# Four graph layers with residual and layer norm: denominators read back behind the last stores, residuals in idle buffers, counts loaded ahead, pieces made by ScalarE

## The chip, the cores and the metric

The kernel runs on one core of a Trainium2 chip. The metric is the device time of one execution in microseconds. The kernel before was run five times: the median is 3411.24 us, the lowest 3408.18, the highest 3414.22. One execution was also profiled; every duration below comes from it.

The engines are called by their short names: PE is TensorE, DVE is VectorE, ACT is ScalarE, POOL is GpSimd and SP is SyncE, which here only issues transfers. PSUM is the memory that PE writes to.

## The reference

`x` is 3327 x 512 in float32, `adj` is 3327 x 3327 of 0 and 1. Four layers follow each other, each of the form `x = layernorm(x + L(x, adj))`:

```python
# layers 0, 2 (8 heads of 64) and 3 (4 heads of 128); layers 2 and 3 end with elu
Wh = x @ W[h];  f1 = Wh @ a1;  f2 = Wh @ a2
e = leaky_relu(f1[:, None] + f2[None, :], 0.2)
att = softmax(where(adj > 0, e, -9e15), axis=1)
L = concat_h(att @ Wh)
# layer 1
keep = (adj > 0) & (cumsum(adj > 0, axis=1) <= 64)
cnt = keep.sum(1)
xj = leaky_relu((keep @ x) / max(cnt, 1) @ Wn.T + bn)
xi = leaky_relu(x @ Wl.T + bl)
L = xi + where(cnt > 0, xj, 0)
```

## The kernel before

**Tiles.** Rows and columns are padded to 26 tiles of 128 (`NT`), and two halves of 13 tiles (`HALF`, 1664 columns, `IW`). The mask (`adj` transposed, fp8) stays in SBUF for all layers. Weighted values go through DRAM (`vd`), as do the unnormalised outputs (`hd`).

**Attention (layers 0, 2, 3).** `Layer.unit` (L361) is one half of the query columns with one of four groups of heads: two heads in layers 0 and 2, one in layer 3. So a layer has eight units, (half, s) = (0, 0) to (1, 3). A unit goes over the 26 key tiles `j`. For each key tile and head, DVE makes the weights `t` from the row terms `rb` and the mask (L402), ACT makes from `t` an fp8 indicator `y`, whether the score is above zero (L405), and PE multiplies `t` with the values `vj` into `po` (L425, from L413). The softmax's denominators are split off: PE sums `y` and the mask against small bf16 "pieces" (`sden`, `sm`) into `pd` (`den`, L375 and L377), two key tiles after the `t`. The pieces are the bf16 parts of the exponentials of the columns, made by `cut` (L321), one call for each half.

**Jobs.** A unit returns a list of small jobs, which the next unit takes one for each key tile: the outputs turned by PE (`pt`, L453), copied by ACT to `hb` (L457) and stored by SP to `hd` (L458). At the end of a half, `pd` holds the sums of all heads; DVE turns it with four transposes into `db` (L486, L487) and reduces it (L491) to `red`. SP writes `red` in four transfers of 32-byte pieces to `dd` (L495) and reads it back in one, with the layout changed, as `pes` (L498); `finish_sums` (L500 on) makes the reciprocals `rec` on DVE from it (L507, L511, L513). The last unit of layer 3 does this with PE instead (`sums`, 13 matmuls with a constant `c1w`, L533). In unit (0, 0) `prepare` and `cut` for the second half are among the jobs, in layer 0 also the counts of neighbours by tile (`count_jobs`, L612: PE counts into `pct`, DVE casts to `ct` at L629, PE sums the tiles before into `pn` at L631, DVE clamps it at L632, stores it to `ctd` and finds the empty columns `nb` at L635). The second half's counts are in unit (0, 2).

**Passages.** `finish_steps` (L165) ends a layer for two row tiles: it loads `h` from `hd` and the residual `xr` (L126 is the line of both loads), divides by `rec` (L180), for elu an exponential `e` (L185), adds (L191, L192, L194), and `norm_rows` (L144) takes the statistics (L152, L153) and scales (`rs` at L154 to L158, `h` at L161). Tiles 0 and 1, which need the first half only, are finished ahead inside the last unit (`ending`, L434).

**Layer 1.** `sage` (L645) has two stages. In the first, for each row tile, PE turns `h` (L682), ACT copies it to `xT` (L684), PE multiplies by both weights (`pz` L690, `pi` L693); `pz` is split into three bf16 parts, of which two, `zs`, stay in SBUF and the third goes through DRAM (`zd`, L700); `xi` is stored (L705). In the second, `kept` (L770, L774) makes the 0/1 tiles `kt` of neighbours to keep from a running count, with carries `cy` loaded by POOL (L659) and added by ACT (L762); PE sums `acc` over 26 key tiles and three parts (L809), the third from `zl`, loaded at L727; `output` (L778) divides by the counts `cnt` (from `cb`, L741 to L745) and finishes a row tile (first step `y`, L782). Layer 2's projection is done between, as jobs, with `wsb` (L730). Layer 3's projection is in `third` (L822 on), with `pt` (L258) and `pw` (L268).

**What sets the order.** PE runs in the order of the program text. For the other engines a scheduler sets a fixed order when the kernel is built, except for instructions pinned by `keep_in_program_order`. Each engine runs its order strictly in turn. Transfers by SP go round eight queues' semaphores, and a transfer may carry a wait for the one eight before it.

Of the kernel before, what the change touches and what calls it, by code (L numbers as in the profile page):

```python
# [18 lines left out]
P = 128  # L19
# [13 lines left out]
def kernel(  # L33
# [131 lines left out]
    def finish_steps(pool, xin, layer, t0, n, hbufs=6, eng=nc.sync, xbufs=None):  # L165
        H, D = layer.H, layer.D
        ys, xs, steps = [], [], []

        def load():
            for t in range(t0, t0 + n):  # L170
                h = pool.tile([P, F], F32, name="h", bufs=hbufs)
                load_tile(h, hd, t, eng)
                ys.append(h)
                xr = pool.tile([P, F], F32, name="xr", bufs=xbufs)
                load_tile(xr, xin, t, nc.gpsimd)
                xs.append(xr)

        def divide(s):
            h = ys[s]
            nc.vector.tensor_tensor(h.rearrange("p (h d) -> p h d", h=H), h.rearrange("p (h d) -> p h d", h=H),  # L180
                                    rec[:, t0 + s, :H].rearrange("p (h e) -> p h e", e=1).to_broadcast([P, H, D]),
                                    op=ALU.mult)
            if layer.elu:
                e = pool.tile([P, F], F32, name="e")
                nc.scalar.activation(e, h, AF.Exp)  # L185
                xs.append(e)

        def add(s):
            h, xr = ys[s], xs[s]
            if layer.elu:  # L190
                nc.vector.scalar_tensor_tensor(xr, xs[n + s], 1.0, xr, op0=ALU.min, op1=ALU.add)  # L191
                nc.vector.scalar_tensor_tensor(h, h, 0.0, xr, op0=ALU.max, op1=ALU.add)  # L192
            else:
                nc.vector.tensor_tensor(h, h, xr, op=ALU.add)  # L194

        steps.append(load)
        for s in range(n):
            steps += [lambda s=s: divide(s), lambda s=s: add(s)]
        steps.append(lambda: norm_rows(pool, ys, t0))
        return ys, steps  # L200
# [22 lines left out]
    class Layer:  # L223
# [97 lines left out]
        def cut(self, pool, half, tag="pc", bufs=1, pinned=False):  # L321
# [7 lines left out]
            for c0 in (0, 3):  # L329
                if c0:  # L330
                    nc.vector.tensor_tensor(dc, dc, qc, op=ALU.mult)
                ins = nc.vector.tensor_copy(pc[:, :, :, c0], dc)
                if pinned:
                    tc.keep_in_program_order(ins)
                nc.vector.tensor_tensor(rest, dc, pc[:, :, :, c0], op=ALU.subtract)
                nc.vector.tensor_copy(pc[:, :, :, c0 + 1], rest)
                nc.vector.tensor_tensor(rest, rest, pc[:, :, :, c0 + 1], op=ALU.subtract)
                nc.vector.tensor_copy(pc[:, :, :, c0 + 2], rest)
# [6 lines left out]
            for k in range(HS):  # L345
                m = self.sm[:, ts, 32 * k:32 * k + 32].rearrange("p t (s c) -> p t s c", c=8)
                for c0, f in ((0, -0.5), (3, -1.0)):
                    nc.vector.tensor_scalar(m[:, :, :, c0:c0 + 3], pc[:, :, k::HS, c0:c0 + 3], f, None,
                                            op0=ALU.mult)
# [11 lines left out]
        def unit(self, pools, half, s, background, aside, final=None, ending=None):  # L361
# [72 lines left out]
            if ending:  # L434
                ending()
# [46 lines left out]
            if not (final and s == NS - 1):  # L482
# [9 lines left out]
                dd = dram.tile([IW, 2, 2 * NS], F32, name=f"dd{self.li}{half}{s}")  # L492
                for kk in range(4):
                    i_, w_ = (0, WA) if kk < 2 else (WA, WB)
                    nc.sync.dma_start(out=dd[i_:i_ + w_, kk % 2, :].rearrange("(b i) x -> i b x", i=32),  # L495
                                      in_=red[32 * kk:32 * kk + 32, :w_ // 32].rearrange("p b o s -> p b (o s)"))
                pes = sp.tile([P, HALF, 2, 2, NS], F32, name="pes", tag="red", bufs=1)
                nc.sync.dma_start(out=pes.rearrange("p q k o s -> p q (k o s)"),  # L498
                                  in_=dd.rearrange("(q p) k x -> p q (k x)", p=P))
# [15 lines left out]
                jobs += [nothing] * max(0, 6 - len(jobs))  # L515
                at = 6 if half == 0 or s < NS - 1 else len(jobs)
                if final and s > 1:

                    return [nothing] * 5 + [finish_sums] + jobs[2:]
                return jobs[:at] + [finish_sums] + jobs[at:]  # L520

            for c in range(2):
                nc.scalar.copy(db[:64, c * (WA // 2):(c + 1) * (WA // 2)], pd[c][:64, :WA // 2])
                nc.vector.tensor_copy(db[64:, c * (WB // 2):(c + 1) * (WB // 2)], pd[c][64:, :WB // 2])
            held = []

            def sums():

                pe = po[0][:, :2 * HALF * H].rearrange("p (q o h) -> p q o h", q=HALF, o=2)
                held.append(pe)  # L530
                for q in range(HALF):
                    e = int(q >= NA)
                    nc.tensor.matmul(pe[:, q, :, :], db[:, (q - e * NA) * P:(q - e * NA + 1) * P], c1w[:, :, e, :],  # L533
                                     start=True, stop=True)

            def reciprocals():
                pe = held[0]
                nc.vector.tensor_tensor(r_[:, :, 0, ss], pe[:, :, 0, ss], rc[:, :, 0, ss], op=ALU.mult)
                nc.vector.tensor_tensor(r_[:, :, 0, ss], pe[:, :, 1, ss], r_[:, :, 0, ss], op=ALU.add)
                nc.vector.reciprocal(rec[:, t0:t0 + HALF, hs], rec[:, t0:t0 + HALF, hs])  # L540


# [69 lines left out]
    def count_jobs(pool, half):  # L612
        jobs = []
        for s0, n in QUADS:
# [12 lines left out]
            def none(i0=i0, w_=w_, held=held):  # L627
                ct = pool.tile([P, 4 * P], BF, name="ct", bufs=1)
                nc.vector.tensor_copy(ct[:, :w_], held["p"][:, :w_])  # L629
# [5 lines left out]
                nc.vector.tensor_scalar(nb[:, :w_], pn[:, :w_], 0.0, None, op0=ALU.is_equal, saturate=False)  # L635
# [9 lines left out]
    def sage(first, first_pool, xin, prev, nxt, wsrc, dst):  # L645
# [3 lines left out]
        with tc.tile_pool(name="sg_z", bufs=1, reuse_waits="tile") as zp, \  # L649
# [20 lines left out]
            with tc.tile_pool(name="sa_w", bufs=1, reuse_waits="tile") as wp, \  # L670
# [35 lines left out]

                pend = None
# [12 lines left out]
            with tc.tile_pool(name="sb_w", bufs=1, reuse_waits="tile") as wp, \  # L720
# [9 lines left out]
                load_wide(wsb, wsrc, nc.gpsimd)  # L730
                nc.vector.tensor_copy(wsb[:, :, :, FW:], wa[nxt.li].rearrange("p c (e h) -> p c e h", e=2))
# [7 lines left out]

                cb = wp.tile([P, NT], BF, name="cb")  # L740
                nc.gpsimd.dma_start(out=cb, in_=ctd[NT:NT + 1, :].rearrange("o (t p) -> p (o t)", p=P))  # L741
                cnt = wp.tile([P, 3, NT], F32, name="cnt")
                nc.vector.tensor_scalar(cnt[:, 0, :], cb, NEIGHBOURS, 1.0, op0=ALU.min, op1=ALU.max)
                nc.vector.reciprocal(cnt[:, 1, :], cnt[:, 0, :])
                nc.vector.tensor_scalar(cnt[:, 2, :], cb, 0.0, None, op0=ALU.is_gt)  # L745
# [53 lines left out]
                for b in range(len(blocks)):  # L799
# [3 lines left out]
                    for s in range(G):  # L803
                        acc = ps.tile([P, F], F32, name="acc", bufs=2)
                        for t in range(NT):
                            if b == 0 and len(kts) < NT and t % 2 == 0:
                                kts += kept(0, len(kts))
                            for c in range(3):
# [7 lines left out]
                            if jobs and (t == 11 and t0 + s > 1 or t == 17):  # L816
                                jobs.pop(0)()
                        y = output(acc, t0 + s)
# [172 lines left out]
    with tc.tile_pool(name="col0", bufs=1) as cp, tc.tile_pool(name="raw", bufs=2) as rawp, \  # L991
# [63 lines left out]
        def first_jobs(pool, half, s):  # L1055
# [6 lines left out]
            if (half, s) == (0, 1):  # L1062
                jobs = []
                for li, wT, a in ((2, w2T, a2), (3, w3T, a3)):
# [10 lines left out]
                     ending=lambda: ends.extend(finish(f0, x, L0, 0, 2, 2)))  # L1075

    with tc.tile_pool(name="col2", bufs=1) as cp:
# [3 lines left out]
        with tc.tile_pool(name="fin2", bufs=1, side="right") as f2:  # L1081
            ends = []
            with tc.tile_pool(name="at_r2", bufs=3, reuse_waits="tile") as rp, \
# [7 lines left out]
                             ending=lambda: ends.extend(finish(f2, x2, L2, 0, 2, 2)))  # L1091
# [47 lines left out]
```

## Time and profile before

| | |
|---|---|
| median of five runs | 3411.24 us |
| profiled execution | 3414.22 us, span 3412.0 us, mean granted PE clock 0.982 |
| layer 0's projection, mask | 0 to 140 us |
| layer 0's attention, 8 units | 140 to 960 us |
| layer 1, first stage | 960 to 1171 us |
| layer 1, second stage, with layer 2's projection | 1171 to 1776 us |
| layer 2's attention | 1776 to 2568 us |
| layer 3's projection | 2568 to 2716 us |
| layer 3's attention | 2716 to 3380 us |
| tail | 3380 to 3412 us |

The stages' borders are read from the first and last instructions of their lines in the timeline. In the rows of groups, a line, an engine, an operation and its tiles come first, then busy time, mean ns of one and the idle time of the engine just before, with what ended it. In a timeline row the start, the duration (of several merged instructions where the count at the end is over one), and in square brackets the idle time ahead of it and what it waited for.

### The profile page before, as it was taken

The numbers are of one execution on the slowest core, as the hardware profiler recorded it, in microseconds if no ns is written. First come the engines' busy times: TensorE is split into PE (matmuls) and PEld (weight loads), VectorE is DVE, ScalarE is ACT, GpSimd is POOL, SyncE is SP. The second block draws the span as 40 slices with busy tenths as digits, with TensorE's granted clock in tenths as the row PEclk, the third lists the DMA queues.
The fourth block names the chain that finished last, engine by engine and source line by source line (L and its number), as shares of the span: only waits on it lengthen the run. The fifth ranks groups of instructions, "written<-read, shape, count | busy, mean of one in ns | idle before, by whom it ended". The sixth has DMA issues, their size and how long they took to land.

```text
span 3412.0 us, 46967 instructions
## 1 busy us (share of the span) xinstructions
PE 3267.9 (96%) x18371; PEld 1633.4 (48%) x18423; DVE 2695.9 (79%) x2630; ACT 2351.8 (69%) x2128; POOL 216.3 (6%) x344
## 2 busy tenths in 40 slices
PE   8899999999989899999989999999997999999997
PEld 7534344444434345545544444444445754445453
DVE  6799999999967544444449999999997766668886
ACT  2388998999943233333338999899996755559885
POOL 3100000000010111111110000000001000000000
PEclk9899999999989999999999999999998999999998
DMA  9544111111143433333320111111107411122311
GB/s 380 208 131 120 49 49 53 46 45 30 36 129 123 124 102 90 87 87 85 83 80 25 42 50 48 56 45 46 35 25 224 169 41 42 41 51 79 95 42 48
DMA packets 313365, 284.65 MB, mean 83 GB/s; under 512 B 134253, under 2 KB 248631, under 8 KB 313144
## 3 DMA queue, kind: packets, MB, share of 16 engines
q1 hardware_dynamic: 280584, 170.27, 17.0%
q0 software_dynamic: 27040, 103.70, 9.7%
q10 hardware_dynamic: 5520, 7.69, 0.7%
q8 instruction: 145, 2.38, 0.3%
q14 instruction: 76, 0.62, 0.1%
HBM read 212.22 MB, written 69.35 MB: 83 GB/s over the span
## 4 chain that ended last, share of the span: by engine, by line
PE 81%; DVE 7%; issue 5%; DMA 4%; ACT 2%; SPq 0%; POOL 0%; ACTq 0%; DVEq 0%; POOLq 0%
PE po L425 49%; PE acc L809 12%; PE pd L377 7%; PE pw L268 5%; DVE t L402 4%; PE pz L690 3%; PE pi L693 3%; DMA raw<-in_adjT_dram 2%; PE pk L770 1%; PE pt L453 1%; ACT y L405 1%; PE pa L1022 0%; PE pt L258 0%; DVE mask L593 0%; DMA cy<-ctd 0%
## 5 line engine op out<-in xcount | busy, mean ns | idle before, releaser
L402 DVE SCALAR_TENSOR_TENSOR t<-rb,qc,mask 128x1664 f32<-128x1664 f32 x1040 | 1959.9, 1960 | 167.4 <-PE po L425 149.9
L405 ACT ACTIVATE y<-t,bi,sc 128x1664 fp8e4<-128x1664 f32 x1040 | 1771.2, 1766 | 317.8 <-PE pd L377 304.9
L425 PE MATMUL po<-t,vj 128*64 128x448 f32 (+3 forms) x8320 | 1927.0, 520 | 25.1 <-DVE t L402 22.2
L425 PEld LDWEIGHTS po<-t,vj 128*64 128x64 f32 (+1 forms) x8320 | 847.7, 148 | 981.4 <-issue 691.6
L809 PE MATMUL acc<-zs,kt 128*128 128x512 bf16 x1312 | 396.9, 382 | 2.2 <-issue 0.2
L809 PEld LDWEIGHTS <-kt 128*128 128x128 fp8e4 x2028 | 199.7, 98 | 252.4 <-issue 11.4
L268 PE MATMUL pw<-wsb,xT 128*128 128x264 f32 (+1 forms) x1248 | 303.4, 399 | 5.8 <-DVE vt L274 4.2
L762 ACT CAST pk<-cy 128x512 f32<-128x512 bf16 x169 | 99.0, 587 | 298.9 <-DVE kt L774 253.1
L268 PEld LDWEIGHTS pw<-wsb,xT 128*128 128x128 f32 x1248 | 242.8, 198 | 51.2 <-ACT qc L272 3.2
L377 PE MATMUL pd<-y,sden 128*32 128x448 fp8e4 (+1 forms) x4160 | 259.3, 341 | 8.2 <-ACT y L405 8.2
L809 PE MATMUL acc<-zl,kt 128*128 128x512 bf16 x664 | 253.1, 381 | 5.6 <-DMA zl<-zd 4.9
L774 DVE SCALAR_TENSOR_TENSOR kt<-pk,mask 128x512 fp8e4<-128x512 f32 x169 | 116.0, 687 | 102.1 <-PE pk L770 102.1
L377 PEld LDWEIGHTS <-sden 128*32 128x32 bf16 x4160 | 117.3, 96 | 160.5 <-issue 137.6
L274 DVE TENSOR_TENSOR vt<-pw,dc 128x256 f32<-128x256 f32 x156 | 59.1, 419 | 145.2 <-ACT dc L269 141.7
L356 POOL DMA_DIRECT2D rb<-r x40 | 21.2, 532 | 1618.6 <-DVE t L402 1604.4
L272 ACT COPY rc<-pw 128x8 f32<-128x8 f32 (+1 forms) x78 | 12.7, 163 | 137.5 <-PE pw L268 137.5
L690 PE MATMUL pz<-wn,xT 128*128 128x512 f32 x208 | 98.7, 619 | 9.1 <-ACT xT L684 9.1
L693 PE MATMUL pi<-wl,xT 128*128 128x512 f32 x208 | 93.5, 592 | 0.0
L659 POOL DMA_DIRECT2D cy<-ctd x91 | 67.9, 746 | 340.4 <-ACT pk L762 312.2
L154 ACT ACT_TABLE_LOAD x45 | 57.7, 1283 | 37.3 <-DVE mv L153 36.7
L782 DVE SCALAR_TENSOR_TENSOR y<-acc,cnt,bnb 128x512 f32<-128x512 f32 x26 | 19.5, 751 | 80.0 <-PE acc L809 80.0
L593 DVE TENSOR_SCALAR mask<-raw 128x832 fp8e4<-128x832 int32 (+2 forms) x90 | 52.9, 598 | 36.1 <-DMA raw<-in_adjT_dram 36.0
(177 smaller groups left out, 1665.5 us busy)
## 6 DMA issues: line engine op xcount, KB each, us to landing
vj<-v SPq DMA_DIRECT2D x312, 128.0 KB
rb<-r POOLq DMA_DIRECT2D x40, 832.0 KB, 4.7
raw<-in_adjT_dram SPq DMA_DIRECT2D x67, 416.0 KB
cy<-ctd POOLq DMA_DIRECT2D x78, 256.0 KB, 4.0
h<-hd SPq DMA_DIRECT2D x61, 256.0 KB
v<-vt SPq DMA_DIRECT2D x50, 256.0 KB
hd<-hb SPq DMA_DIRECT2D x48, 256.0 KB
xr<-x POOLq DMA_DIRECT2D x45, 256.0 KB, 3.2
```

The costliest lines, as they stand in the source:

```text
L268: nc.tensor.matmul(pw[e][:, :FW + H], xT[:, c, :], wsb[:, c, e, :], start=c == 0, stop=c == FC - 1)
L274: nc.vector.tensor_tensor(vt[:, hs, :], pw[e][:, :FW].rearrange("p (h d) -> p h d", d=D), self.dc[:, t, hs].rearrange("p (h e) -> p h e", e=1)
L377: nc.tensor.matmul(pd[c][32 * kk:32 * kk + 32, :w_], lhsT, rhs, start=(kk, c) not in seen, skip_group_check=final is not None, stop=last a ...
L402: nc.vector.scalar_tensor_tensor(t, rb[k], self.qc[:, j, h:h + 1], mask[:, j, i0:i0 + IW], op0=ALU.max, op1=ALU.mult)
L405: nc.scalar.activation(y, t, AF.Sigmoid, bias=self.bi[:, j, h:h + 1], scale=self.sc[:, j, h:h + 1], saturate=False)
L425: nc.tensor.matmul(po[c][k * D:(k + 1) * D, :z - a_], vj[:, j % 2, k * D:(k + 1) * D], ts[k][:, a_:z], start=j == 0, stop=j == NT - 1)
L659: nc.gpsimd.dma_start(out=cy[:, :n, :], in_=ctd[t:t + n, b * GW:(b + 1) * GW] .rearrange("(o t) i -> o t i", o=1).to_broadcast([P, n, GW]))
L690: nc.tensor.matmul(pz, xT[:, c, :], wn[:, c, :], start=c == 0, stop=c == FC - 1)
L693: nc.tensor.matmul(pi, xT[:, c, :], wl[:, c, :], start=c == 0, stop=c == FC - 1)
L762: nc.scalar.copy(pks[k % 2], carry[b, t // 4 * 4][:, t % 4:t % 4 + 2, :])
L774: nc.vector.scalar_tensor_tensor(kt, pk, NEIGHBOURS, mask[:, t:t + 2, i0:i0 + GW], op0=ALU.is_le, op1=ALU.mult, saturate=False)
L809: nc.tensor.matmul(acc, kts[t][:, s * P:(s + 1) * P], zs(t, c) if c < 2 else zl[:, t, :], start=t == 0 and c == 0, stop=t == NT - 1 and c ...
```

## The change

- The reduced sums `red` are written to `dd` in one transfer of 128 rows of 896 bytes. The read-back `pes` is 16 transfers of 32-byte pieces. They are issued by a job of their own (`place`): at the end of a layer 0 or 2 on SP behind the last stores `hd`, else on POOL.
- At the end of half 0 of layers 0 and 2, `pd` is copied to `db` by ACT, PE sums it with 13 matmuls (`sums`, as layer 3's last unit does), and DVE makes the reciprocals from PSUM.
- The residuals `xr` of tiles 0 and 1 are loaded into buffers of the tag `hb`, and `e` has two buffers at the end of layer 2.
- In layer 1 the counts `cb` and `cnt` are loaded and made in the first stage; the weights `wsb` are loaded by SP after the first `acc`; the first output's `zl` matmuls come after all its `zs` matmuls.
- In `cut`, the casts `pc` and the scalings `sm` are done by ACT; so is the cast `ct` of the counts, and `nb` reads `ct` in place of `pn`.

```diff
 def finish_steps(...):
-                xr = pool.tile([P, F], F32, name="xr", bufs=xbufs)
+                xr = xpool.tile([P, F], F32, name="xr", tag="hb") if xpool else \
+                    pool.tile([P, F], F32, name="xr", bufs=xbufs)
-                e = pool.tile([P, F], F32, name="e")
+                e = pool.tile([P, F], F32, name="e", bufs=ebufs)
 def cut(...):
-                ins = nc.vector.tensor_copy(pc[:, :, :, c0], dc)
+                ins = nc.scalar.copy(pc[:, :, :, c0], dc)
...
-                    nc.vector.tensor_scalar(m[:, :, :, c0:c0 + 3], pc[:, :, k::HS, c0:c0 + 3], f, None,
-                                            op0=ALU.mult)
+                    nc.scalar.mul(m[:, :, :, c0:c0 + 3], pc[:, :, k::HS, c0:c0 + 3], f)
 def unit(...):
-            if not (final and s == NS - 1):
+            by_pe = HS == 2 and half == 0 or final and s == NS - 1
+            if not by_pe:
...
-                for kk in range(4):
-                    i_, w_ = (0, WA) if kk < 2 else (WA, WB)
-                    nc.sync.dma_start(out=dd[i_:i_ + w_, kk % 2, :].rearrange("(b i) x -> i b x", i=32),
-                                      in_=red[32 * kk:32 * kk + 32, :w_ // 32].rearrange("p b o s -> p b (o s)"))
+                nc.sync.dma_start(out=dd, in_=red.rearrange("p b o s -> p b (o s)"))
-                nc.sync.dma_start(out=pes.rearrange("p q k o s -> p q (k o s)"),
-                                  in_=dd.rearrange("(q p) k x -> p q (k x)", p=P))
+                end = half == 1 and s == NS - 1
+                def place():
+                    for kk in range(4):
+                        q0, nq = (0, NA) if kk < 2 else (NA, HALF - NA)
+                        src = dd[32 * kk:32 * kk + 32, :4 * nq].rearrange("i (q m) x -> m i q x", m=4)
+                        for m in range(4):
+                            ins = (nc.sync if end else nc.gpsimd).dma_start(
+                                out=pes[32 * m:32 * m + 32, q0:q0 + nq, kk % 2].rearrange("p q o s -> p q (o s)"), in_=src[m])
...
+                if end:
+                    return jobs + [place, finish_sums]
                 if final and s > 1:
-                    return [nothing] * 5 + [finish_sums] + jobs[2:]
+                    return [nothing, nothing, place, nothing, nothing, nothing, finish_sums] + jobs[2:]
+                jobs += [nothing] * max(0, 7 - len(jobs))
+                return jobs[:2] + [place] + jobs[2:7] + [finish_sums] + jobs[7:]
...
-                nc.vector.tensor_copy(db[64:, c * (WB // 2):(c + 1) * (WB // 2)], pd[c][64:, :WB // 2])
+                (nc.scalar.copy if HS == 2 else nc.vector.tensor_copy)(
+                    db[64:, c * (WB // 2):(c + 1) * (WB // 2)], pd[c][64:, :WB // 2])
...
+            if not final:
+                return jobs[:2] + [sums, nothing, reciprocals] + jobs[2:]
 def count_jobs(...):
-                nc.vector.tensor_copy(ct[:, :w_], held["p"][:, :w_])
+                nc.scalar.copy(ct[:, :w_], held["p"][:, :w_])
-                nc.vector.tensor_scalar(nb[:, :w_], pn[:, :w_], 0.0, None, op0=ALU.is_equal, saturate=False)
+                nc.vector.tensor_scalar(nb[:, :w_], ct[:, :w_], 0.0, None, op0=ALU.is_equal, saturate=False)
 def sage(...):
-                            for c in range(3):
+                            for c in range(2 if t0 + s == 0 else 3):
...
+                        if t0 + s == 0:
+                            for t in range(NT):
+                                nc.tensor.matmul(acc, kts[t][:, :P], zl[:, t, :], start=False, stop=t == NT - 1)
+                            load_wide(wsb, wsrc, nc.sync)
+                            nc.vector.tensor_copy(wsb[:, :, :, FW:], wa[nxt.li].rearrange("p c (e h) -> p c e h", e=2))
```

The loads of `cb` and the three instructions for `cnt` move in the text from the start of `sage`'s second stage to before the first stage's loop; the old load of `wsb` on POOL goes.

## The prediction

> **What bounds the kernel now.** I read the engine totals, then the busy time by stretch, then the timeline where TensorE (PE) has gaps. The totals of the page:
>
> ```profile
> PE 3267.9 (96%) x18371; PEld 1633.4 (48%) x18423; DVE 2695.9 (79%) x2630; ACT 2351.8 (69%) x2128; POOL 216.3 (6%) x344
> L402 DVE SCALAR_TENSOR_TENSOR t<-rb,qc,mask 128x1664 f32<-128x1664 f32 x1040 | 1959.9, 1960 | 167.4 <-PE po L425 149.9
> ```
>
> PE idles 144 us in all, but 96% is a mean over stages. Windows, columns PE, PEld, DVE, ACT, POOL, PE clock, DMA share, GB/s:
>
> ```profile
> 562.00:659.00 97.00, 95.09 (x681) 42.54 (x677) 96.88 (x61) 86.43 (x58) 0.73 (x2) 1.00 0.15 43
> 2264.00:2361.00 97.00, 96.19 (x703) 41.76 (x702) 97.00 (x53) 90.43 (x61) 1.06 (x2) 1.00 0.15 45
> 2800.00:2900.00 100.00, 100.00 (x379) 49.82 (x378) 64.90 (x37) 54.92 (x33) 0.53 (x1) 1.00 0.21 47
> 960.00:980.00 20.00, 9.14 (x28) 4.51 (x27) 5.16 (x15) 4.87 (x10) 3.45 (x8) 0.66 0.89 253
> 1180.00:1200.00 20.00, 14.68 (x50) 5.83 (x50) 4.88 (x10) 4.12 (x7) 3.77 (x6) 0.74 1.02 269
> 2560.00:2580.00 20.00, 8.91 (x86) 5.51 (x83) 11.87 (x24) 13.83 (x20) 9.39 (x14) 0.82 0.64 199
> 2580.00:2600.00 20.00, 11.77 (x37) 9.26 (x36) 13.60 (x31) 8.69 (x16) 2.35 (x5) 0.67 0.88 252
> ```
>
> Layers 0 and 2's attention (first two rows) has no gap on DVE: a unit is 52 `t` starting 1.862 us apart, 96.85 us, and PE is only about 1 us behind it (97.00 - 96.19). Layer 3 (third row) is PE's alone. The last four rows are the three passages between stages, where PE does 9 to 15 us of work in 20. So a microsecond off DVE pays in layers 0 and 2 until PE is full; one off a passage's chain pays whole; in layer 3 neither pays. What ends the passages' waits:
>
> ```profile
> 963.10 9.64 SPq L495 DMA_DIRECT2D dd<-red  x4
> 973.57 6.22 PE L690 MATMUL pz<-wn,xT 128*128 128x512 f32 x8 [9.11 <-ACT xT L684]
> 986.29 1.11 PE L682 MATMUL pt<-ident,h 128*128 128x128 f32 x4 [3.06 <-ACT h L161]
> 1180.77 0.59 PE L809 MATMUL acc<-zl,kt 128*128 128x512 bf16 x1 [4.94 <-DMA zl<-zd]
> 1190.45 0.18 DVE L743 TENSOR_SCALAR cnt<-cb 128x26 f32<-128x26 bf16 x1 [6.65 <-DMA cb<-ctd]
> 2586.72 0.21 DVE L507 SCALAR_TENSOR_TENSOR rec<-pes,rc 128x52 f32<-128x52 f32 x1 [5.64 <-DMA pes<-dd]
> 2593.90 1.11 PE L258 MATMUL pt<-ident,h 128*128 128x128 f32 x4 [8.23 <-ACT h L161]
> ```
>
> **The change part by part** (+ is time gained).
>
> *Pieces and counts on ACT, layer 0.* In unit (0,0) DVE loses six casts and four scalings (0.39 us each in their rows, but they overlap: by start to start about 2.0 us), three wide and one narrow `ct` (next start 0.60 us later, narrow 0.29: 2.1 us), and `nb` reads SBUF instead of PSUM (between nothing and 0.9 us): 4 to 5 us. New waits: DVE's `rest` waits for ACT's `pc`, and behind it stand `t` and the mask casts, for which PE's `po` waits; PE's `pn` waits for ACT's `ct`, with `po` behind it. ACT's `y` is in front of each with 1.77 us, and ACT is 16.9 us busy of 20 there, so a wait may cost up to 1.8 us, six or seven times over, though a `t` usually stands between. From -2 to +5; I take +2.5, half of what DVE loses. The second half's counts, unit (0,2), come where PE is 96.66 of 97.00 busy (368 to 465), so 2.1 to 3 us off DVE give +0.5 (0 to 2).
>
> *Denominators of half 0 by matmul, layers 0 and 2.* The four transposes (567.32 to 569.85) and two reductions (571.72 to 572.61) leave DVE: 3.4 us in each of two units, which take 96.85 + 3.4 = 100.3 us. Five small DVE instructions of the same sort as the old reciprocals stay. PE gains 13 matmuls of 128x16; the nearest row is line 533's 128x8, 26 instructions (13 matmuls in two passes) in 3.21 us at half to two thirds of the clock, so 1.6 to 3.2 us. PE's own minimum in a unit is 96.19 x 26/26.05 = 96.0 us, which makes 97.6 to 99.2. ACT gains four copies of 0.5 to 0.6 us, in a unit with 86.4 of 97 busy: covered by `y`'s lead of two key tiles over `pd`; if that cover is gone, PE waits 2.2 us. Gain 1.1 to 2.7 twice; bounds 0 and 3.4 each. I take +4 for both (0 to 7).
>
> *From layer 0 to layer 1.* `dd` goes out in one transfer, but its landing is not what PE waits for: that is ACT's `xT`, behind the copy `hb` that waited 8.44 us for the store before the last to land (972.1), beside 2 MB of weights. That stays. After the change ACT's order has `rs` of tiles 2 and 3 ahead of `xT` of tiles 0 and 1. That `rs` needs tile 3's statistics, which stand on DVE behind the first `rec<-pes`; and the 16 `pes` transfers are issued on SP only after the last `hd`, the second eight each behind the landing of one of the first eight. Eight issues at 0.36 to 0.5 us from 974, about 3 us to land (the one old `pes` took 2.56 from issue to use), and the same again: about 981, and 1.5 us of DVE and ACT work before `xT`. So PE starts near 982 instead of 973.6: -8.5. Back come the wait of 3.06 us at 986.29 (tiles 2 and 3 are ready by then) and the slow clock behind it, where `pz` took 6.15 us against 3.60 at full clock: 2.5 us, in sum 5.6. Tiles 4 and 5 may lose it again: their `h` loads come behind the 16 on SP, and the moved `cnt`, which waits for `cb` (11.65 us from issue to landing in the old place), stands on DVE ahead of tile 5's sum. I take -4 (-12 to +2).
>
> The Trainium skill, "TensorE: Matmul & The Clock Gate", Part 1, puts the fall to half clock at an idle window of about 3.4 us, free-running. Taken strictly, a 3.06 us wait would leave the clock up and 2.5 us fewer would come back here, so this step would be -6.5; the trace shows the slow `pz` behind that very wait, and I go by it.
>
> *Inside layer 1.* Now PE waits 4.94 us for `zl`, then DVE 6.65 us for `cb`, and between them the carries `cy`, behind `wsb`, `bnb` and `cb` on POOL. After it `cb` and `cnt` are done long before, `cy` is POOL's first transfer, `wsb` goes out on SP after the first output, and the 26 `zl` matmuls of the first output come last. These cost 26 x 0.2165 = 5.6 us wherever they stand. `kt` for 26 key tiles then is 13 steps; from 1175.6 ten more at 1.5 us (their pace at 1199 to 1204) with some 3 us for late carries end near 1194, and the `zl` at 1199.6. The first output now is at 1207.98: +8.4. If `zl`'s 3.4 MB hold the carries up (a carry took up to 7.6 us here), +5; if not, +12. The `wsb` load has two outputs' time before its first use: nothing.
>
> *Into layer 2 and its first unit.* The pieces of half 0 become a chain of ACT and DVE in turn: +0.2 (-1 to +1). Those of half 1 take 3.9 us off DVE and put about 3 back with their waits: +0.8 (-1 to +2).
>
> *From layer 2 to layer 3.* Now the second residual's buffer comes late (`xr` and `e`), PE waits 10.85 us until 2579.07, then 8.23 us until 2593.90 for tile 2, which waits for `rec<-pes` at 2586.72, though its own half's `rec` was long done: it only stands behind it on DVE. With a second `e` and `xr` in the idle `hb` both tiles finish early; first `pw` 2 us sooner. Of tiles 2 and 3 all but the reciprocal `rs` stands ahead of the wait, and `pes`, no longer behind an `h` load on SP, arrives by 2583 or so even in two trains. Tile 2 near 2589: +5 (2 to 8, and below nothing in the second rival).
>
> *Layer 3.* PE has no gap, so neither the `pes` transfers on POOL (16 x 0.54 = 8.6 us, one slot of the loads `rb`) nor sums five slots later move the end; if `rec` comes late, DVE (64.9 of 100) has room. -0.5 (-3 to +1). The tail is as it was.
>
> Sum: 2.5 + 0.5 + 4 - 4 + 8.4 + 0.2 + 0.8 + 5 - 0.5 = +16.9. The profiled execution took 3414.2 (span 3412.0 and 2.2 around it): 3397.3 after. It is 3.0 above the median of 3411.24, so the median goes to **3394**.
>
> **The rivals.**
> 1. *PE and ACT keep what DVE gives.* For it: PE is 1 to 2 us behind DVE in each attention unit. Against it: the two units with transposes last 3.4 us longer than the others. The 7 us of the attention are nothing then: 16.9 - 7 = 9.9, about 3401.
> 2. *The read-back takes the place of every wait removed* (slower). 32-byte pieces of `dd` are now read in 16 transfers instead of written in four. In quiet the four landed in 2.08 us (572.73), beside the weights in 9.64 and 8.37 us (963.10 and 2571.75). Two trains at 9.6 us put `rec` near 993 and near 2593: PE starts at 995 (-22, 5 back: -17), tile 2 of layer 3's projection at 2599 (-5). Sum 16.9 - 13 - 10 = -6, median 3417. Each microsecond per landing costs about four, so the sign turns near 3 + 17/4 = 7 us a landing. Against it: the weights have landed by 973 in the first passage.
> 3. *Bounds fall well*: 3.4 us in both units, `pes` in 2 us, carries in time: about 3380.
> 4. *The parts cancel*, or the moved transfers meet others so that the first output of layer 1 comes no sooner: near 3409.
>
> The skill's "DMA: Bandwidth & Descriptors", section "Anatomy of one DMA", gives a fixed cost of about 2 us to a transfer, mostly its completion. Two trains would then be an estimated 4 us of pure landing against my 6, and the passage out of layer 0 would cost 2 us less.
>
> **How the numbers follow.** Forecast 0.47; rival 1 0.20; rival 2 0.15; rival 3 0.10; rival 4 0.08. A measurement tells 0.2% (6.8 us) from no change. Faster by that: 0.47, 0.14 of rival 1 and 0.10: 0.71. Within: 0.06 + 0.05 + 0.06 = 0.17. Slower: 0.10 of rival 2 and 0.02: 0.12. Range: the forecast's terms, mostly independent, give 3384 to 3404; with rival 1 and parts of 3 and 4, 3378 to 3410.
>
> **What would show it.** Right: `cnt` no longer waits for `cb`, the first `y` of layer 1 comes 26 us or so after its first `kt` instead of 34; units (1,0) of layers 0 and 2 last 97.5 to 99.5 us; tile 2 at the start of layer 3 waits under 5 us. The first `pz` of layer 1 should come 6 to 10 us later after the last `po` than now; if not, I mis-read ACT's order. Wrong: `rec<-pes` more than 12 us behind the last `hd`; PE waiting for `db` or for `pc`-bound `t` in layer 0's first unit; an idle PE in layer 3 with `rec` as releaser.

## The result, and the profile after

The changed kernel takes 3413.63 us (median of 25 runs, 3408.83 to 3419.11); the kernel before took 3409.75 in the runs beside it (45 runs). The ratio is 1.0011, 95% interval 1.0006 to 1.0017: no change by the 0.2% bound, slightly slower by its own interval, where 3394 was forecast. The profiled executions differ by as little (spans 3412.3 and 3412.0), so their stages can be set against each other. One caution: the profiled execution of the kernel before (3414.22) lies 4.5 us above its median, that of the changed kernel (3413.99) within 0.4 us of its own, so the table shows none of the 3.9 us between the medians. Each boundary is an instruction's start or end in the timelines.

| stage | before, us | after, us | gained | forecast |
|---|---|---|---|---|
| start to layer 0's first `t` | 141.08 | 145.98 | -4.9 | 0 |
| unit (0,0), to the next unit's first `pt` | 130.65 | 132.68 | -2.0 | +2.5 |
| to (0,2)'s first `pt` | 104.20 | 105.04 | -0.8 | 0 |
| to (0,3)'s first `pt` | 102.39 | 99.80 | +2.6 | +0.5 |
| to (1,1)'s first `pt` (denominators by matmul) | 198.38 | 196.55 | +1.8 | +2 |
| to layer 0's last `pd` | 282.87 | 285.01 | -2.1 | -4, with the next |
| last `pd` to the last `pi` of layer 1 | 212.11 | 215.87 | -3.8 | |
| last `pi` to first `kt` | 2.20 | 2.10 | +0.1 | 0 |
| first `kt` to first `y` of an output | 34.10 | 32.11 | +2.0 | +8.4 |
| to layer 2's first `t` | 568.15 | 567.25 | +0.9 | +0.2 |
| layer 2, first unit | 115.98 | 117.81 | -1.8 | +0.8 |
| to (1,1)'s first `pt` (denominators by matmul) | 391.93 | 388.52 | +3.4 | +2 |
| to layer 2's last `pd` | 282.09 | 282.10 | 0.0 | 0 |
| last `pd` to the last `pw` of layer 3 | 144.72 | 143.13 | +1.6 | +5 |
| to the last `pt`; to the end | 677.52; 23.63 | 675.44; 22.91 | +2.8 | -0.5 |

The page's totals after the change, and the passages that the prediction showed (windows: PE, PEld, DVE, ACT, POOL, clock, DMA share, GB/s):

```profile
PE 3253.3 (95%) x18423; PEld 1625.0 (48%) x18475; DVE 2673.7 (78%) x2554; ACT 2374.4 (70%) x2198; POOL 239.8 (7%) x390
```

```profile
960.00:980.00 20.00, 6.04 (x57) 4.34 (x47) 7.14 (x14) 8.92 (x11) 6.72 (x10) 0.75 0.66 215
980.00:1000.00 20.00, 10.51 (x23) 4.85 (x24) 9.06 (x26) 5.09 (x9) 1.63 (x3) 0.66 0.56 114
1180.00:1200.00 20.00, 12.52 (x40) 4.58 (x40) 8.08 (x14) 5.75 (x10) 4.13 (x6) 0.83 0.84 236
2570.00:2590.00 20.00, 7.66 (x46) 5.72 (x35) 12.21 (x26) 10.26 (x18) 7.30 (x13) 0.69 0.73 235
```

DVE did lose 22 us of work and the span did not shorten; the passages are as empty as they were. The timeline of the changed kernel says what took the place of each wait:

```profile
85.72 1.23 PE L310 MATMUL pr<-ident,rc 128*8 128x128 f32 x5 [5.38 <-ACT rr L312]
185.36 0.59 PE L648 MATMUL pn<-ct,below 128*128 128x512 bf16 x1 [3.55 <-ACT ct L646]
964.52 0.54 PE L377 MATMUL pd<-y,sden 128*32 128x448 fp8e4 x6 [3.07 <-ACT y L405]
979.00 9.18 SPq L504 DMA_DIRECT2D pes<-dd  x16
987.60 0.22 DVE L515 SCALAR_TENSOR_TENSOR rec<-pes,rc 128x52 f32<-128x52 f32 x1 [10.00 <-DMA pes<-dd]
989.49 5.80 PE L707 MATMUL pz<-wn,xT 128*128 128x512 f32 x8 [20.07 <-ACT xT L701]
1195.06 1.11 ACT L778 CAST pk<-cy 128x512 f32<-128x512 bf16 x2 [5.00 <-DMA cy<-ctd]
2582.30 0.27 ACT L457 COPY hb<-pt 128x128 f32<-128x128 f32 x1 [5.27 <-DMA hd<-hb]
2583.33 1.97 PE L259 MATMUL pt<-ident,h 128*128 128x128 f32 x8 [10.44 <-ACT h L161]
2594.32 0.21 DVE L515 SCALAR_TENSOR_TENSOR rec<-pes,rc 128x52 f32<-128x52 f32 x1
2596.56 0.66 PE L259 MATMUL pt<-ident,h 128*128 128x128 f32 x4 [3.75 <-ACT h L161]
```

The first two are ACT's new work; the third is an order: with both residuals early, ACT's fixed order has `rs` of tiles 0 and 1 ahead of the last `y`. The next three are the read-back and what stands behind it. Then the carries: `cnt` no longer waits (it runs at 992.92), but ACT now waits longer for `cy`. The last four are the passage to layer 3. Its first wait is almost as long as the 10.85 us of before: `h` of tiles 0 and 1 stands on ACT behind the last copy `hb`, which waits for a store. Its second wait is shorter than the 8.23 us of before, and `rec` there shows no wait for `pes`.

### The profile page after: what moved, and what is told of

Same layout as the page of the kernel before. It is cut to its first block, busy times and chain, and to the rows that moved or that the text cites. A ratio compares the mean times of both kernels' runs of the same rounds, so it can differ in the third digit from the quotient of the medians.

```text
span 3412.3 us, 47106 instructions
## 1 busy us (share of the span) xinstructions
PE 3253.3 (95%) x18423; PEld 1625.0 (48%) x18475; DVE 2673.7 (78%) x2554; ACT 2374.4 (70%) x2198; POOL 239.8 (7%) x390
## 5 line engine op out<-in xcount | busy, mean ns | idle before, releaser
L425 PEld LDWEIGHTS po<-t,vj 128*64 128x64 f32 (+1 forms) x8320 | 838.2, 148 | 978.6 <-issue 709.1
L826 PE MATMUL acc<-zl,kt 128*128 128x512 bf16 x638 | 241.8, 379 | 0.6
L273 ACT COPY rc<-pw 128x8 f32<-128x8 f32 (+1 forms) x78 | 13.1, 168 | 141.8 <-PE pw L269 134.8
```

What stands on the lines that cost most here:

```text
L425: nc.tensor.matmul(po[c][k * D:(k + 1) * D, :z - a_], vj[:, j % 2, k * D:(k + 1) * D], ts[k][:, a_:z], start=j == 0, stop=j == NT - 1)
L826: nc.tensor.matmul(acc, kts[t][:, s * P:(s + 1) * P], zs(t, c) if c < 2 else zl[:, t, :], start=t == 0 and c == 0, stop=t == NT - 1 and c ...
```

## The experiments

The theories, each with its rival in the expectations: **A**, ACT is the wrong engine for the pieces and the counts' cast; **B**, the denominators' read-back costs the passages more than it frees, through what stands behind it; **C**, the early residuals change what overtakes what at layer 2's end and win nothing; **D**, in layer 1 the wait for the counts covered one for the carries.

Ratios are to the kernel before, with 95% intervals; the changed kernel has 1.0011. Stage times are from each run's profile.

**Parts of the changed kernel undone, and one buffer more.**

`u_act`: the changed kernel with `cut` and `ct` on DVE again.

```diff
-                ins = nc.scalar.copy(pc[:, :, :, c0], dc)
+                ins = nc.vector.tensor_copy(pc[:, :, :, c0], dc)
...
-                nc.scalar.copy(ct[:, :w_], held["p"][:, :w_])
+                nc.vector.tensor_copy(ct[:, :w_], held["p"][:, :w_])
```

> The changed kernel with the pieces' casts and scalings and the counts' cast back on DVE (nb still reads ct). Theory A (ACT is the wrong engine for them): in layer 0's projection PE no longer waits 5.4 us for the copy rr behind the casts, so the first t comes 2.7 to 4.9 us sooner; in unit (0,0) PE no longer waits 3.5 us for ct, 2 to 3 us sooner; unit (0,2) loses its 2.6 us again and layer 2's first unit 0.5. Sum: 3 to 5 us faster than the changed kernel, 3409 to 3411 by the median. Rival (the moves were worth what I forecast and the projection's 4.9 us are the DMA's chance): 3 to 5 us slower, near 3417.

0.9998 (0.9990 to 1.0007): 4.4 us faster than the changed kernel. Layer 0 starts at 141.34, unit (0,0) takes 129.22, (0,2) goes back to 101.53, layer 2's first unit to 115.95. Theory A as a whole; which of the two moves did it is told apart below.

`u_dd`: the changed kernel with the four writes and the one read-back of before.

```diff
-                nc.sync.dma_start(out=dd, in_=red.rearrange("p b o s -> p b (o s)"))
+                for kk in range(4):
+                    i_, w_ = (0, WA) if kk < 2 else (WA, WB)
+                    nc.sync.dma_start(out=dd[i_:i_ + w_, kk % 2, :].rearrange("(b i) x -> i b x", i=32),
+                                      in_=red[32 * kk:32 * kk + 32, :w_ // 32].rearrange("p b o s -> p b (o s)"))
...
+                nc.sync.dma_start(out=pes.rearrange("p q k o s -> p q (k o s)"),
+                                  in_=dd.rearrange("(q p) k x -> p q (k x)", p=P))
+                place = nothing
```

> The changed kernel with the denominators' old way: four writes, one read-back, right behind each other ahead of the last stores; sums at their new slots. Theory B (the 16 read-backs and ACT's order behind them cost the passage out of layer 0 about 10.7 us of which 6.7 come back): the first pz follows the third hb by about 1.5 us instead of 12.1, but tiles 2 and 3 are late again; net 3 to 5 us faster at the end of layer 1's first stage, layer 3's projection within 2 us: median 3408 to 3411. Rival (the transfers are hidden, the loss is the weights' later landing): no difference, 3412 to 3415.

1.0010 (1.0001 to 1.0019): no difference from the changed kernel. The first `pz` comes sooner (16.0 us behind the last `pd` instead of 24.4), but the stage behind it is longer by almost as much (199.1 against 191.4), so 0.8 us is left. By this run alone the rival's outcome, no difference, is what came.

`u_xr`: the changed kernel with the residuals in their old buffers.

```diff
-                     ending=lambda sp: ends.extend(finish(f0, x, L0, 0, 2, 2, nc.sync, None, sp)))
+                     ending=lambda sp: ends.extend(finish(f0, x, L0, 0, 2, 2)))
...
-                             ending=lambda sp: ends.extend(finish(f2, x2, L2, 0, 2, 2, nc.sync, None, sp, 2)))
+                             ending=lambda sp: ends.extend(finish(f2, x2, L2, 0, 2, 2)))
```

> The changed kernel with the residuals of tiles 0 and 1 back in their own buffers, e with one. Theory C (early residuals let the 1 MB of wsb overtake the stores hd, whose landing then ends the passage out of layer 2, so that nothing is won): the last hb falls back from 11.5 to some 7.5 us behind the last pd, and the first pw comes within 2 us of the changed kernel's; total within 2 us, 3412 to 3416. Rival (the residuals' early load was worth the 5 us I gave it, and something else took it): 4 to 6 us slower, 3418 to 3420.

1.0024 (1.0015 to 1.0032): 4.4 us slower than the changed kernel. Layer 0's last unit is back at 282.87 (the late `y` is the residuals' doing), but the passage to layer 3 takes 146.7 instead of 143.1 and the one to layer 1 218.5 instead of 215.9. Theory C is out for the changed kernel: there, early residuals help. The size is uncertain, as the stages are from an execution 4 us above this kernel's median.

`cy3`: the changed kernel with a third buffer for the carries.

```diff
-                cy = cyp.tile([P, 4, GW], BF, name="cy")
+                cy = cyp.tile([P, 4, GW], BF, name="cy", bufs=3)
```

> The changed kernel with three buffers instead of two for the carries cy of layer 1. Theory D (in the first output of layer 1 the wait for cb was covered by the wait for carries, which two buffers cannot fetch ahead of zl's 3.4 MB; ACT now waits 17 us for them there): the first y comes 5 to 8 us sooner after the first kt (32.1 now), total 5 to 8 us faster, 3406 to 3409. Rival (the DMA engines are full with zl and a third buffer only queues): under 2 us.

1.0018 (1.0010 to 1.0027), not faster; yet the stage that it is about did what theory D says: first `kt` to first `y` in 25.87 us instead of 32.11. ACT's waits in that stretch, in the changed kernel and here (waits view: us in total, times, longest):

```profile
ACT pk L778 <- DMA cy<-ctd: 17.1, 6, 5.0
```

```profile
ACT pk L778 <- DMA cy<-ctd: 7.7, 2, 4.3
```

The 6 us were lost again 200 us earlier. With the buffers changed, the scheduler put DVE's `rec<-pes` ahead of all work on tiles 2 and 3, and layer 1's first stage, from the last `pd`, took 222.9 us:

```profile
987.01 0.21 DVE L515 SCALAR_TENSOR_TENSOR rec<-pes,rc 128x52 f32<-128x52 f32 x1 [22.14 <-DMA pes<-dd]
1000.26 1.12 PE L699 MATMUL pt<-ident,h 128*128 128x128 f32 x4 [12.49 <-ACT h L161]
```

DVE idles 22 us in front of one instruction that tiles 2 and 3 do not need, and PE waits for them. (The profiled execution is the fastest of this kernel's twelve, 8 us under their median, so its stages explain where time went but not the whole ratio.) A changed buffer count turned an order 200 us away, so a run's total says little about the line that was edited: the stage has to be looked at.

**Parts alone on the kernel before.**

`p_sage` is the kernel before with the changed function `sage`; `p_xr` with the changed `xr` and `e` of `finish_steps` and the two `ending` lines.

> The kernel before with the changes inside layer 1 alone (counts ahead, weights after the first output, zl sums last). Theory D (the carries bound the first output): it comes 2 us sooner after the first kt, 32 instead of 34.1, as in the changed kernel, and the early cb costs the first stage 0 to 2 us; total 0 to 2 us faster than before. Rival (the stage's gain was cut by what the other parts do ahead of it): the 8 us of the forecast appear.

> The kernel before with the residuals of the last tiles in the idle buffers alone. At layer 0's end ACT's order takes rs ahead of the last y: the last pd comes 2.1 us later after the last unit's start. At layer 2's end, last pd to end of layer 3's projection: 141 instead of 144.7 if the early residuals are what helps (3.6, from the difference of two runs), 144 to 145 if they help only together with the rest. Total 0 to 2 us faster than before.

`p_sage` 1.0006 (0.9997 to 1.0015): first `kt` to first `y` 32.7, and 213.8 instead of 212.1 in the first stage. The part is worth nothing measurable as it stands; the carries bound it without any help from the other parts: between 1160 and 1215 us ACT waits 16.5 us for them in `p_sage`, and 9.2 in the kernel before. `p_xr` 0.9998 (0.9988 to 1.0007): layer 0's last unit 285.06, so +2.2 as expected; the passage to layer 3 139.4.

That passage needs care. In kernels whose residuals are the old ones it took 141.1 to 146.7 us, also where nothing near it was changed (144.7 before, 141.3 in `p_sage`); with the new ones 139.4 to 143.7. The part's 5 us are not established; the two groups' means (five and twelve profiles) lie 1.6 us apart.

`p_cut` is the kernel before with the changed function `cut`; `p_pe` with `by_pe`, the copies to `db` and the changed `sums` and `reciprocals`:

```diff
-            if not (final and s == NS - 1):
+            by_pe = HS == 2 and half == 0 or final and s == NS - 1
+            if not by_pe:
...
+            if not final:
+                return jobs[:2] + [sums, nothing, reciprocals] + jobs[2:]
```

> The kernel before with the pieces' casts and scalings on ACT alone. If they are what cost the changed kernel its start: layer 0's projection 3 to 4.5 us longer, unit (0,0) 3 to 3.5 us longer, layer 2's first unit 0 to 2: 6 to 9 us slower than before. If they cost only beside the other parts: within 2 us of before.

> The kernel before with half 0's denominators of layers 0 and 2 by matmul alone. By the changed kernel's stages: 1.9 us in layer 0, 3.4 us in layer 2: 4 to 6 us faster than before. If PE or ACT is the next bound without the other parts: 0 to 2.

`p_cut` 1.0028 (1.0016 to 1.0039): 9.5 us slower, the largest effect of a part alone. Its waits of PE in layer 0's projection:

```profile
PE pt L258 <- DMA xt<-in_x_dram: 9.9, 3, 4.3
PE pr L309 <- ACT rr L311: 5.5, 1, 5.5
```

Before, the second line is 0.5 us. The casts stand in ACT's order ahead of the copies `rr`, each pair waits for a DVE result in between, and `pr` has PE's next `pw` behind it. Layer 0's attention starts at 144.1 to 146.0 us in the six runs with the pieces on ACT and at 141.1 to 143.3 in the eleven others (means 145.1 and 142.2; the 141.08 of before is the lowest): 2.9 us, and the rest of the 4.9 in the table lies within the spread. Unit (0,0) takes 134.80, 4.2 more, and layer 2's first unit 118.3, 2.4 more. The same stretch of that unit, before and here:

```profile
157.00:177.00 20.00, 17.84 (x142) 7.12 (x138) 19.97 (x30) 12.17 (x12) 0.00 (x0) 0.91 0.26 69
```

```profile
160.00:180.00 20.00, 17.84 (x143) 7.16 (x139) 15.86 (x12) 12.74 (x17) 0.00 (x0) 0.91 0.09 21
```

PE does the same work in both. Its chain (`pr` waits twice for `rr`, which waits for a store) sets the pace there, and the casts had lain in time that DVE would otherwise have waited: taken away, DVE is idle for 4 us. The pieces are ready later, and the rest of their work on DVE meets the counts: 14 `t` after the first, both kernels are at 31 us, four `t` on `p_cut` is 5.0 us behind. The three stages named add up to 9.6 us, as the ratio has it. The two profiles still have the same span, 3412.0: that of `p_cut` is one of its two fastest, 5 us under its median, and the other stages, those with loads, are shorter in it.

`p_pe` 0.9986 (0.9977 to 0.9995): 4.7 us faster; (0,3) to (1,1) 196.5 in layer 0, 388.6 instead of 391.9 in layer 2.

**Combinations.** `combo` is the changed kernel with `cut` and the first half's `ct` on DVE, the old transfers of the denominators, layer 0's residuals in their own buffers, `cb` loaded in the fifth pair of tiles, and three carry buffers. `combo_dd` has the changed kernel's transfers instead.

```diff
-            def none(i0=i0, w_=w_, held=held):
+            def none(i0=i0, w_=w_, held=held, copy=nc.scalar.copy if half else nc.vector.tensor_copy):
...
-                nc.scalar.copy(ct[:, :w_], held["p"][:, :w_])
+                copy(ct[:, :w_], held["p"][:, :w_])
...
                 for t0 in range(0, NT, 2):
+                    if t0 == 8:
+                        tc.keep_in_program_order(nc.gpsimd.dma_start(
+                            out=cb, in_=ctd[NT:NT + 1, :].rearrange("o (t p) -> p (o t)", p=P)))
```

> The changed kernel with: pieces and first half's counts back on DVE (second half's on ACT), the denominators' old transfers, layer 0's residuals in their own buffers, cb loaded in the fifth pair of tiles, three buffers for the carries. From the stages measured so far: unit (0,0) -1.4, (0,2) -2.6, denominators by matmul -5.3, first output of layer 1 -8, layer 2 to 3 -4, layer 3 -1.8, the rest as before: 20 to 24 us faster than before. If the stages' gains are not additive (an order that the scheduler turns round), 5 to 15.

> The same with the changed kernel's one write and sixteen read-backs. Theory B: the passages out of layers 0 and 2 cost 3 to 10 us more than in the run beside it, in waits behind rec and pes; layer 3 the same. Rival: within 1.5 us of it.

`combo` 0.9958 (0.9944 to 0.9972), 14 us faster than before, in the lower of the two ranges I expected; `combo_dd` 0.9987 (0.9978 to 0.9996), 10 less. From the last `pd` to the end of layer 1's first stage `combo` takes 214.6, `combo_dd` 220.8; that is 6.2 of the 10, and no other stage differs as much. DVE's wait for `pes` and PE's waits there, first `combo`, then `combo_dd`:

```profile
974.31 0.21 DVE L513 SCALAR_TENSOR_TENSOR rec<-pes,rc 128x52 f32<-128x52 f32 x1 [15.75 <-DMA pes<-dd]
PE pt L697 <- ACT h L161: 7.4, 2, 6.1
```

```profile
979.25 0.21 DVE L516 SCALAR_TENSOR_TENSOR rec<-pes,rc 128x52 f32<-128x52 f32 x1 [20.24 <-DMA pes<-dd]
PE pt L700 <- ACT h L161: 12.0, 2, 10.7
```

Counted from the last `pd`, `rec` comes 4.5 us later in `combo_dd`, and so does what stands behind it.

`combo_ct` and `combo_cut` are `combo` with one thing on ACT again: `ct` of the first half (`nc.scalar.copy` for both halves), and the changed function `cut`. Both also copy `rc` into `rec` ahead of the sums at the ends of layers 0 and 2, a small edit that the later runs share.

> The combination with the counts' cast on ACT in the first half too. Theory A, split: unit (0,0) of layer 0 takes 2 to 3.5 us longer than the combination's 129.9, nothing else changes: 2 to 3.5 us slower.

> The combination with the pieces and their scalings on ACT, counts as in it. Theory A, split: layer 0's projection ends 3 to 4.5 us later (142 to 145 or 146), unit (0,0) 0 to 2 later, layer 2's first unit 1.8 later: 5 to 8 us slower. If the projection's 4 us are the chance of the mask's transfers, 2 to 4.

`combo_ct` 0.9962 (0.9948 to 0.9975): my expectation fell. Unit (0,0) takes 127.39, 2.5 us less than in `combo`: the counts' cast on ACT is a gain there, though none shows in the ratio. PE has no wait for `ct` in that unit, so the 3.55 us in the changed kernel came with the pieces ahead of it in ACT's queue. `combo_cut` 0.9990 (0.9981 to 0.9999), 11 us slower than `combo` and more than the 5 to 8 that I expected: start at 145.07, (0,0) 133.26, layer 2's first unit only 0.2 more. By the two profiles it is 6.6 us.

`late` and `late_dd` are built on `combo` and make the sums at the ends of layers 0 and 2 three pairs of tiles later, with another buffer for `pes`, `late_dd` with the changed kernel's transfers, `late` with the old ones there and the new ones in layer 3 alone.

```diff
-                    return jobs + [place, finish_sums]
+                    self.finish_sums = finish_sums
+                    return jobs + [place]
...
                 for t0 in range(0, NT, 2):
+                    if t0 == 6:
+                        prev.finish_sums()
...
+                    if t0 == 6:
+                        L2.finish_sums()
```

> The fastest combination so far, with the sums at the ends of layers 0 and 2 made only after four more pairs of tiles (tiles 2 to 12 don't need them), the old transfers read back behind the last stores there, and the new transfers in layer 3 alone. Theory B (not the transfers but what stands behind rec on DVE is what costs): PE's 7.4 us of waits for h in layer 1's first stage go, pd to the end of that stage falls from 214.6 to about 206; the passage to layer 3 by 2 to 5; layer 3 to 667.7. 10 to 14 us faster than the combination, near 3384 where before is 3410. Rival (tiles 2 and 3 then wait for their own loads behind the weights): 3 to 5.

> The same with one write and sixteen read-backs at the ends of layers 0 and 2 too. Theory B: the sixteen now cost only what stands behind them on SP (loads h of tiles 4 on): within 3 us of the run beside it. Rival (the 32-byte transfers themselves slow the others): 5 to 10 us slower than it.

`late` 0.9966 (0.9953 to 0.9978), `late_dd` 0.9968 (0.9956 to 0.9979). Two readings. First, with nothing behind `rec`, the sixteen read-backs cost nothing that the ratios show (2.1 us in layer 1's first stage, by the profiles), against 10 us in `combo_dd`: their price was the order behind them. Second, the 10 us and more that I expected over `combo` are not there, nor the rival's 3 to 5: PE still waits 4.5 us for `h` in `late`, and the first stage takes 212.7. What the rival named is in the trace of `late`: DVE now waits for the loads of `h`,

```profile
977.47 1.29 DVE L181 TENSOR_TENSOR h<-h,rec 128x512 f32<-128x512 f32 x2 [8.19 <-DMA h<-hd]
```

but no run took that wait away.

`best` is `late` with `ct` on ACT in both halves.

> The late sums (old transfers at the ends of layers 0 and 2, new ones in layer 3) with the counts' cast on ACT in both halves: 2.5 us less in unit (0,0), the rest as in the run with late sums: 13 to 17 us faster than before.

0.9953 (0.9941 to 0.9965), 16 us faster than before and as expected, (0,0) 127.83, first `kt` to first `y` 27.4. It is the fastest by its median ratio; its interval overlaps those of `combo` and `combo_ct`.

## Why the prediction was wrong

The forecast had +16.9, the two profiles give -0.3. Of the 17 us:

- **The pieces and counts on ACT** (+3.3 forecast for the start and the two first units, -8.7 in the table, the largest miss) were priced too well, and one of their places not at all. I took half of what DVE loses as gain in unit (0,0), and did not price `cut` for half 0 in layer 0's projection: there it costs 2.9 us, in unit (0,0) 3.4 to 4.2 (the counts alone give 2.5 back in `combo_ct`), in layer 2's first unit 0.2 to 2.4. `p_cut`: 9.5 us in all. The failed step was "a microsecond off DVE pays in layers 0 and 2 until PE is full": that was read from units without jobs and used in one where PE's chain through `rr` sets the pace for 20 us. That "a wait may cost up to 1.8 us" failed too: it priced the one `y` in front, and PE's wait for `ct` in that unit was 3.55 us. The whole queue on ACT was the thing to list (`rr`, then `ct`), since PE waits for it in order.
- **Inside layer 1**: +8.4 forecast, +2.0 measured. The mis-sized term is "some 3 us for late carries"; ACT waits 17.1 us for them, and waited 9.2 in the kernel before already. With a third buffer the stage takes 25.9, close to the 25.7 that I had forecast; so the two loads taken off the path were priced about right, with some luck, since ACT still waits 7.7 us for carries there. The waits for `zl` and `cb` had hidden a part of the one for the carries.
- **Layer 0 to layer 1**: -4 forecast, -5.9 measured. The mechanism was right (ACT's `rs` ahead of `xT`, behind `rec`, behind sixteen transfers): -8.5 forecast for the start of `pz` behind the `hb` copies, -10.7 measured, since SP takes 0.57 us on average for each of the sixteen and I had 0.36 to 0.5; 5.6 to come back, 6.7 came. The late last `y`, 2.1 us, I did not see, though ACT's order of the changed kernel showed it.
- **Layer 2 to layer 3**: +5 forecast, +1.6 measured. The step that failed is "first `pw` 2 us sooner". Counted from the last `pd`, the first `pw` starts after 16.2 us where it was 14.8, since the last copy `hb`, with tiles 0 and 1 behind it on ACT, waits 5.27 us for its store and runs at 11.5 us instead of 7.5. In `u_act`, `u_dd` and `cy3` it is as late; in `p_xr` it runs at 5.2 and the first `pw` at 13.1, 1.7 us sooner than before and nearly as forecast. Why that store is late in the changed kernel stays open. The reciprocals came 23.5 us behind the last `pd` where before it was 20.6 and I had some 17; but `rec` shows no wait for `pes` there, so the sixteen read-backs are not shown to be why. How much the residuals alone give stays open (1.6 us by the groups above, and `u_xr` says 3.6).
- **Denominators by matmul**: +4 forecast, 5.2 by the stages, 4.7 by `p_pe`. Right.
- **Second half's counts** +2.6 against +0.5, **layer 3 and the tail** +2.8 against -0.5. I had capped the first by PE's 96.66 of 97 busy, but that was not PE's need: the profile has PE busy for 101.12 of the unit's 102.39 us before and for 98.87 of 99.80 after, with the same matmuls. The second is open: the kernels with the new transfers take either 675.4 to 676.3 or 677.1 to 677.4 there, the others 676.2 to 678.3.

By its number rival 2 came nearest (3417), by what happened rival 4: parts that cancel, though it had 3409. Rival 2's mechanism was there out of layer 0, at less than its price. That price was misread: 2.08, 9.64 and 8.37 us are the times in which SP issued the four transfers, its own waits included, and not their landings. Rival 1's (PE and ACT keep what DVE gives) held for the pieces and not for the denominators. Of the signs, `cnt` without a wait, units (1,0) of 99.59 and 97.94 us by their `t`, and a wait of 3.75 us for tile 2 came much as forecast; the first `y` after 32.1 us instead of 26 did not.

On the two rules cited: I had taken the slow clock behind a wait of 3.06 us from the trace, against a strict reading of the Trainium skill's "TensorE: Matmul & The Clock Gate", Part 1. In the changed kernel that wait is gone and `pz` runs in 3.60 us there, so the 2.5 us came back as the trace had it. `u_dd` has `pz` at 6.08 us behind a wait of 3.69, which is beyond that page's window of about 3.4 us and fits both. The granted clock supports the trace: before, it is 1.00 during the `pi` ahead of the short wait (979.60 to 983.20), 0.87 in the wait and 0.50 behind it (986.29 to 990.00). A wait of this length does not always do it at once: behind 3.08 us in front of the last `pd`, `u_dd` has 0.50 (964.00 to 964.90), and behind 3.07 us the changed kernel still has 1.00 (964.50 to 965.00). On the two microseconds of completion in "DMA: Bandwidth & Descriptors", section "Anatomy of one DMA": the first ten of the sixteen go out 0.65 us apart and the last six 0.48, with no pause at the ninth, so issuing took the time and no landing shows between the trains. That section has its figure for transfers issued by GpSimd; these went out on SP, so the figure itself was not put to the test.

## What to carry to other kernels

An instruction moved to an idle engine enters that engine's order: list what stands behind it there and who waits for that, for every call of the function, also the one in a stage that seemed unconcerned. When one wait is removed, price the next one from its own rows with its buffers (here two carries in flight), not as a remainder: the rows of before had 9.2 us for the carries. And a value that is needed late (`rec` of the second half) should be consumed late in the program text, or a fixed order will put everything behind its transfer.

## What was not expected of the hardware

SP issued sixteen transfers of 32 rows with 32-byte pieces in 9.18 us, 0.57 each on average (9.13 at the end of layer 2), where the four larger ones before took 2.08 us in quiet, 0.52 each. The end of layer 2's attention, where little is loaded, repeats to 0.1 us between kernels (from (1,1)'s first `pt` to the last `pd` 282.1 in all seventeen profiles). Stages with large loads differ for the same code, by 2.2 us at the start (eleven profiles) and by 5.6 in the passage to layer 3 (five), which is what hides small gains there.
